# Attention with a modulated norm, followed by a GRU, on one core: the first part loads by halves of the features and projects q and k of batch 0 by contraction chunks

## The chip, the cores and the metric

The kernel runs on 1 core of a Trainium2 chip. The metric is the device time of one execution in microseconds (us); the number that counts is the median over several runs. Nothing else runs on the chip. All data are float32.

## The reference

There are 16 batches of 256 steps with 512 features, a condition vector of 512 features for each batch, and two layers one after the other.

```python
# layer 0: RMS norm, scaled and shifted by the condition, then attention with 16 heads of 32
scale, shift = split(cond @ W_emb + b_emb)           # W_emb: 512 x 1024
xn  = rms_norm(x, g_norm) * (1 + scale) + shift
q, k, v = split(xn @ W_qkv)                          # W_qkv: 512 x 1536
q, k = rms_norm_per_head(q, g_q), rms_norm_per_head(k, g_k)
o   = softmax(q @ k.T * 32**-0.5) @ v
x   = x + o + o @ W_out
# layer 1: GRU over the 256 steps, its first state is the condition
r = sigmoid(i_r + h_r); z = sigmoid(i_z + h_z); n = tanh(i_n + r * h_n)
h = (1 - z) * n + z * h                              # i = x_t @ W_ih + b_ih, h_* = h @ W_hh + b_hh
out = x + all h
```

## The kernel before

The program has three parts. The **first part** (lines 573 to 660) loads weights and x, makes scale and shift from the condition, and takes batch 0 as far as the start of its attention. The **attention part** loops over the batches 0 to 14 and, in each, over four groups of four heads; one group is one slot (`slot0` to `slot3`), and `last_batch` does batch 15. The **GRU part** runs over the 256 steps. Between the first two parts there is no barrier: the first logits of batch 0 (`logits`, line 285) are the border.

TensorE (PE), VectorE (DVE), ScalarE (ACT) and GpSimd (POOL) execute in the order in which the code is written (`manual_schedule`, line 571), each in its own queue. Each instruction waits for the semaphores of what it needs and holds up everything behind it on its engine. Loads are issued from the queues of SyncE (SP) and of ACT. The loads share eight semaphores in rotation, so that a load waits, before it is issued, until the load that last used its semaphore has landed; loads behind it on its queue wait with it.

What happens to one batch b, with the names that the change touches:

- `load_x(b)` loads x of the batch, 512 KB. The tile has two buffers.
- `norm_first(b)` takes squares and their sum on ACT, one instruction for each of the two halves of the steps (n = 0, 1). The squares themselves are a by-product, written into `xs`. `Rsqrt.first` and `Rsqrt.second` make 1/sqrt out of the sum: Ln and Exp on ACT, then a refinement of three small DVE instructions.
- `norm_apply(b)` writes the normed x into `xs` (DVE, two instructions); then `load_x(b + 2)` is issued.
- `turn_x(b)` transposes `xs` on PE into two PSUM banks, 16 instructions; `put_x` applies scale and shift (`ada_a`, `ada_s`) on the way to `xnT`, one bank by DVE and one by ACT or DVE.
- `project(b, n, s, ks)` multiplies `xnT` by `wq`: half n of the steps, s = 0, 1, 2 for q, k, v, over the contraction chunks ks of 128 features. One call over all four chunks appears in the profile as 32 matmuls (two for each instruction) at line 220. The result takes one PSUM bank.
- `Stats.square` and `Stats.add` square q or k (ACT) and sum by heads (DVE, line 235); `norm_qk` scales (DVE, line 246), `turn_qk` transposes on PE (line 194), `put_qk` writes qT and kT (lines 267 and 269), `put_v` keeps v.

There are eight PSUM banks, A, X, Y, Z and lg0 to lg3; `logits` needs lg0 to lg3. A bank that is given to a new tile waits until the last reader of the old one is done.

In the first part before, the queue of SP holds half of `we` (W_emb, 2 MB in all; ACT's queue holds the other half), x of batch 0, q's columns of `wq` (1 MB), four small rows, k's columns, x of batch 1, v's columns. PE's order is: turn the condition, all of `ps_emb` (the product of condition and `we`, line 587), turn x of batch 0, q and k of half 0, turn x of batch 1, q and k of half 1, with the turning of half 0's q and k and of x of batch 2 behind them, v of half 0, the turning of half 1's q and k, a quarter of v of half 1, the first logits.

Of the kernel before, what the change touches and what calls it, by code (L numbers as in the profile page):

```python
# [8 lines left out]
F32 = mybir.dt.float32  # L9
AF = mybir.ActivationFunctionType  # L10
# [9 lines left out]
def kernel(  # L20
# [52 lines left out]
    for k in range(KC):  # L73
        nc.scalar.dma_start(cond_sb[k * B : (k + 1) * B, :], cond[:, k * P : (k + 1) * P])
# [16 lines left out]
    we = wpool.tile([P, KC, 2 * D], F32, tag="w_a", name="we")  # L91
    for k in range(KC):
        (nc.sync, nc.scalar)[k % 2].dma_start(we[:, k, :], w_emb[k * P : (k + 1) * P, :])
# [3 lines left out]
    def load_x(b):  # L97
        xt = p2.tile([P, NT, D], F32, tag="x", name=f"x_{b}")
        nc.sync.dma_start(xt, x[b].rearrange("(n p) d -> p n d", p=P))
        x_tiles[b] = xt  # L100
# [3 lines left out]
    rows_b = p1.tile([26, P], F32, tag="qkn", name="rows_b", bufs=4)  # L104

    wq = wpool.tile([P, KC, 3 * D], F32, tag="w_b", name="wq")
    for i in range(3):
        for k in range(KC):
            nc.sync.dma_start(
                wq[:, k, i * D : (i + 1) * D], w_qkv[k * P : (k + 1) * P, i * D : (i + 1) * D]  # L110
            )
        if i == 0:
            for r, g in ((0, g_q), (1, g_k)):
                nc.sync.dma_start(
                    rows_b[r : r + 1, :].rearrange("o (i d) -> o i d", d=DH),
                    g.rearrange("(o i d) -> o i d", o=1, i=1).to_broadcast([1, HG, DH]),
                )
            nc.sync.dma_start(rows_b[2:14, :], b_ih.rearrange("(m c) -> m c", c=P))
            nc.sync.dma_start(rows_b[14:26, :], b_hh.rearrange("(m c) -> m c", c=P))
        if i == 1:  # L120
            load_x(1)
# [9 lines left out]
    def tile_ps(name, bank, shape=(P, D)):  # L131
        pool = ps if len(bank) == 1 else ps_lg
        return pool.tile(list(shape), F32, tag=bank, name=name)
# [31 lines left out]
    def norm_first(b, parts=range(NT)):  # L165
        if parts[0] == 0:
            batches[b].xs = p1.tile([P, NT, D], F32, tag="xs", name=f"xs_{b}")
            batches[b].ssx = small.tile([P, NT], F32, tag="ssx", name=f"ssx_{b}")
            batches[b].rs = Rsqrt(batches[b].ssx, D, NT, f"x{b}")
        for n in parts:  # L170
            nc.scalar.activation(
                batches[b].xs[:, n, :], x_tiles[b][:, n, :], AF.Square,
                accum_out=batches[b].ssx[:, n : n + 1],
            )

    def norm_apply(b, rstd):
        for n in range(NT):
            nc.vector.tensor_scalar(
                batches[b].xs[:, n, :], x_tiles[b][:, n, :], rstd[:, n : n + 1],
                None, ALU.mult,  # L180
            )
        batches[b].xnT = p1.tile([P, KC, T], F32, tag="xnT", name=f"xnT_{b}", bufs=2)
        if 0 < b and b + 2 < B:
            load_x(b + 2)
# [52 lines left out]
    def put_v(b, n, a):  # L237
        if n == 0:
            batches[b].v = p2.tile([P, NT, D], F32, tag="v", name=f"v_{b}")
        nc.scalar.copy(batches[b].v[:, n, :], a)  # L240
# [150 lines left out]
    def slot0(b, w, prev, st):  # L391
        m = b + 1
        if b == 0:

            project(b, 1, 2, range(1, KC), st.v1)
            maxima(w, range(HG))
            exps(w, range(HG))
            put_v(b, 1, st.v1)
            st.q = project(m, 0, 0, range(KC), "A")
            for r in range(R):  # L400
                put_x(2, r, st.tpx)
            st.s0 = Stats(m, 0)
            st.s0.add(0, st.s0.square(0, st.q))
            st.k = project(m, 0, 1, (0, 1), "X")
            normalize(w)
            return
# [164 lines left out]
    with tc.manual_schedule(engines=ORDERED):  # L571
# [6 lines left out]
        pe = tile_ps("ps_emb", "Z", (P, 8 * 32))  # L578
        nc.vector.memset(pe, 0.0)
        tp = tile_ps("tp_h0", "X", (P, KC, B))  # L580
# [4 lines left out]
        for k in range(KC):  # L585
            for j in range(4):
                nc.tensor.matmul(
                    pe[32 * j : 32 * j + B, :],
                    h0T[:, k, :],
                    we[:, k, :].rearrange("p (m j c) -> p j m c", j=4, c=32)[:, j],  # L590
                    start=(k == 0),
                    stop=(k == KC - 1),
                )
        tp = tile_ps("tp_rows", "Y")
        nc.tensor.transpose(tp[:, :12], rows, ident[:12, :12])
        norm_first(0)
        batches[0].rs.first()
        norm_apply(0, batches[0].rs.second())
        nc.vector.tensor_copy(cols[:, :12], tp[:, :12])
        emb = p1.tile([P, 8, 32], F32, tag="sq", name="emb")  # L600
        nc.vector.transpose(emb.rearrange("p m b -> p (m b)"), pe)
        nc.vector.tensor_tensor(
            emb[:, :, 0:B], emb[:, :, 0:B], cols[:, 0:8].unsqueeze(2).to_broadcast([P, 8, B]),
            ALU.add,
        )
        nc.vector.scalar_tensor_tensor(
            ada_a, emb[:, 0:KC, 0:B], 1.0, cols[:, 8:12].unsqueeze(2).to_broadcast([P, KC, B]),
            ALU.add, ALU.mult,
        )
        nc.vector.tensor_copy(ada_s, emb[:, KC:, 0:B])  # L610
# [6 lines left out]
        tpx = turn_x(0, "AX")  # L617
        for c in range(KC):
            put_x(0, 0, tpx, (c,))
            put_x(0, 1, tpx, (c,), nc.scalar)  # L620
        norm_first(1)
        batches[1].rs.first()
        norm_apply(1, batches[1].rs.second())
        q = project(0, 0, 0, range(KC), "Y")
        k = project(0, 0, 1, range(KC), "Z")
        tpx = turn_x(1, ("lg0", "lg1"))
        tp = tile_ps("tp_rows_b", "lg3")
        nc.tensor.transpose(tp[:, :26], rows_b, ident[:26, :26])
        nc.vector.tensor_copy(cols[:, 12:], tp[:, :26])
# [5 lines left out]
        s0 = Stats(0, 0)  # L635
        s0.add(0, s0.square(0, q))
        put_x(1, 1, tpx, engine=nc.scalar)
        s0.add(1, s0.square(1, k))
        s0.rs.first()
        put_x(1, 0, tpx)  # L640
        norm_first(2)
        qk = norm_qk(0, 0, (q, k), s0.rs.second())
        batches[2].rs.first()
        q = project(0, 1, 0, range(KC), "A")
        s1 = Stats(0, 1)
        s1.add(0, s1.square(0, q))
        norm_apply(2, batches[2].rs.second())
        k = project(0, 1, 1, range(KC), "X")
        tq = turn_qk(0, 0, qk, ("lg0", "lg1"))
        st.tpx = turn_x(2, "YZ")  # L650
        v = project(0, 0, 2, range(KC), "lg2")
        s1.add(1, s1.square(1, k))
        s1.rs.first()
        put_qk(0, 0, tq, nc.vector)
        put_qk(0, 1, tq, nc.scalar)
        put_v(0, 0, v)
        qk = norm_qk(0, 1, (q, k), s1.rs.second())
        tq = turn_qk(0, 1, qk, ("lg0", "lg1"))
        st.v1 = project(0, 1, 2, (0,), "X")
        put_qk(1, 0, tq, nc.vector)  # L660
        put_qk(1, 1, tq, nc.scalar)

# [293 lines left out]
```

## Time and profile before

| | us |
|---|---|
| median of 3 runs (1765.43 to 1771.71) | 1770.87 |
| the profiled execution | 1754.42 |
| its span, first to last instruction | 1752.6 |
| PE busy | 1729.9 (99%) |
| DVE busy | 1056.8 (60%) |
| ACT busy | 739.5 (42%) |
| start of the first product with `wq` | 16.55 |
| start of the first logits | 40.93 |

The span is one execution by the hardware profiler. "Busy" counts the time in which an engine has an instruction under way. PEld is the loading of weights into the array, which overlaps the matmuls. The chain of waits follows the work back from the last instruction to what released each step; an engine that this chain never leaves sets the time.

### The profile page before, as it was taken

What the parts mean: (1) busy time and instruction counts of PE and PEld (TensorE: products, weight loads), DVE (VectorE), ACT (ScalarE), POOL (GpSimd) and SP (SyncE); (2) the same over time, 40 slices, a digit from 0 to 9 for tenths busy, and PEclk for the clock granted to TensorE, in tenths of its full rate; (3) what the DMA queues carried; (4) which work ended last, traced back from release to release, by engine and by line L of the source; (5) the groups of instructions that cost most, each with busy time, mean ns of one, the idle gap of its engine ahead of it and who ended that gap; (6) DMA issues with size and microseconds to landing.
All of it is one profiled execution on the core that took longest, in us unless ns stands there. A gap on an engine that the chain in (4) does not pass through costs nothing.

```text
span 1752.6 us, 103775 instructions
## 1 busy us (share of the span) xinstructions
PE 1729.9 (99%) x46955; PEld 1355.0 (77%) x46955; DVE 1056.8 (60%) x3324; ACT 739.5 (42%) x2690; POOL 315.5 (18%) x773
## 2 busy tenths in 40 slices
PE   7999999999999999999999999999999999999998
PEld 2444444444444589999999999999999999999997
DVE  4777777777776745555555555555555555555554
ACT  3777777777777722222222222222222222222222
POOL 0344443444334410000000000000000000000000
PEclk9999999999999899999999999999999999999999
DMA  8100000000000111101110111011101100000000
GB/s 287 28 14 14 14 27 14 14 14 14 14 2 2 73 28 20 19 17 19 24 19 17 21 23 18 17 21 22 19 17 21 24 17 17 16 11 11 11 16 16
DMA packets 146266, 44.48 MB, mean 25 GB/s; under 512 B 137899, under 2 KB 138031, under 8 KB 145823
## 3 DMA queue, kind: packets, MB, share of 16 engines
q1 hardware_dynamic: 145351, 36.73, 9.2%
q8 instruction: 368, 6.03, 1.4%
q10 hardware_dynamic: 472, 1.10, 0.2%
q14 instruction: 75, 0.61, 0.1%
HBM read 29.41 MB, written 8.39 MB: 22 GB/s over the span
## 4 chain that ended last, share of the span: by engine, by line
PE 96%; DVE 2%; ACT 1%; DMA 1%; issue 0%; DVEq 0%; ACTq 0%
PE qkv L220 19%; PE gn L775 19%; PE gr L775 19%; PE gz L775 19%; PE o L719 6%; PE lg L285 4%; PE tpa L194 4%; PE o L364 4%; PE tpqk L194 1%; ACT attn L307 1%; PE tpx L194 1%; PE first L520 0%; DMA x<-in_x_dram 0%; DMA we<-in_L_cond_W_emb_dram 0%; DVE trh L799 0%
## 5 line engine op out<-in xcount | busy, mean ns | idle before, releaser
L220 PE MATMUL qkv<-wq,xnT 128*32 128x512 f32 x3072 | 357.6, 600 | 0.6 <-DVE xnT L212 0.6
L318 POOL TENSOR_SCALAR attn<-attn,rden 128x256 f32<-128x256 f32 x510 | 232.8, 478 | 383.1 <-DVE rden L315 262.9
L873 ACT ACTIVATE r<-trr 128x64 f32<-128x64 f32 x256 | 65.4, 256 | 515.6 <-DVE trr L799 515.6
L307 ACT ACTIVATE attn<-lg,neg 128x256 f32<-128x256 f32 x512 | 234.4, 483 | 67.8 <-DVE neg L301 45.1
L799 DVE STREAM_TRANSPOSE trr<-gr 128x128 f32<-128x128 f32 x256 | 81.1, 317 | 247.5 <-PE gr L775 247.4
L220 PEld LDWEIGHTS qkv<-wq,xnT 128*32 128x32 f32 x3072 | 87.6, 110 | 183.4 <-issue 158.9
L877 ACT ACTIVATE n<-n 128x64 f32<-128x64 f32 x256 | 65.7, 257 | 309.8 <-DVE n L876 306.8
L301 DVE TENSOR_REDUCE neg<-lg 128x2 f32<-128x512 f32 x256 | 159.2, 684 | 50.4 <-PE lg L285 50.4
L799 DVE STREAM_TRANSPOSE trh<-gn 128x128 f32<-128x128 f32 x256 | 81.1, 317 | 142.2 <-PE gn L775 142.2
L775 PE MATMUL gn<-wih,xT 128*32 128x128 f32 x4096 | 159.7, 273 | 0.0
L719 PE MATMUL o<-oT,wo 128*32 128x256 f32 x1920 | 148.0, 379 | 0.0
L775 PE MATMUL gr<-whh,padded 128*32 128x128 f32 x4096 | 135.9, 273 | 2.3 <-DVE padded L906 1.4
L908 POOL TENSOR_TENSOR y<-xT,padded 128x64 f32<-128x64 f32 x128 | 41.0, 321 | 533.5 <-DVE padded L906 533.5
L775 PE MATMUL gr<-wih,xT 128*32 128x128 f32 x4096 | 136.1, 273 | 0.0
L775 PEld LDWEIGHTS gn<-wih,xT 128*32 128x32 f32 x4096 | 120.4, 110 | 20.3
L775 PE MATMUL gz<-wih,xT 128*32 128x128 f32 x4096 | 136.0, 273 | 0.0
L775 PE MATMUL gz<-whh,padded 128*32 128x128 f32 x4096 | 135.8, 273 | 0.0
L775 PE MATMUL gn<-whh,padded 128*32 128x128 f32 x4096 | 135.7, 273 | 0.0
L775 PE MATMUL gr<-whh,h 128*16 128x128 f32 x4064 | 134.6, 273 | 0.3
L775 PE MATMUL gz<-whh,h 128*16 128x128 f32 x4064 | 134.2, 273 | 0.2
L775 PE MATMUL gn<-whh,h 128*16 128x128 f32 x4064 | 134.2, 273 | 0.0
L775 PEld LDWEIGHTS gr<-wih,xT 128*32 128x32 f32 x4096 | 117.4, 110 | 20.5
(122 smaller groups left out, 2731.4 us busy)
## 6 DMA issues: line engine op xcount, KB each, us to landing
x<-in_x_dram SPq DMA_DIRECT2D x16, 512.0 KB, 4.0
xin<-in_x_dram SPq DMA_DIRECT2D x256, 32.0 KB, 2.5
out_dram<-osb SPq DMA_DIRECT2D x248, 32.0 KB, 1.9
wq<-in_L_cond_W_qkv_dram SPq DMA_DIRECT2D x12, 256.0 KB, 4.8
wih<-in_L_cond_W_ih_dram SPq DMA_DIRECT2D x4, 768.0 KB
whh<-in_L_cond_W_hh_dram SPq DMA_DIRECT2D x4, 768.0 KB
we<-in_L_cond_W_emb_dram SPq DMA_DIRECT2D x2, 512.0 KB, 4.8
we<-in_L_cond_W_emb_dram ACTq DMA_DIRECT2D x2, 512.0 KB
```

The costliest lines, as they stand in the source:

```text
L194: nc.tensor.transpose(dst[r], src[q], ident[q, q])
L220: nc.tensor.matmul(a[32 * j : 32 * j + 32, :], batches[b].xnT[:, k, n * P + 32 * j : n * P + 32 * j + 32], wq[:, k, s * D : (s + 1) * D], ...
L285: nc.tensor.matmul(w.lg[i][:, n, :], qT[r, g, n * P : (n + 1) * P], kT[r, g, :], start=True, stop=True,)
L301: nc.vector.tensor_reduce(w.neg[:, i, :], w.lg[i], AX.X, ALU.max, negate=True)
L307: nc.scalar.activation(a[:, n, :], w.lg[i][:, n, :], AF.Exp, bias=w.neg[:, i, n : n + 1], accum_out=w.den[:, i, n : n + 1],)
L318: engine.tensor_scalar(w.attn[i][:, n, :], w.attn[i][:, n, :], w.rden[:, i, n : n + 1], 1.0, ALU.mult, ALU.mult,)
L364: nc.tensor.matmul(w.o[i * DH : (i + 1) * DH, :], v[:, k, h * DH : (h + 1) * DH], w.attnT[:, i, k, :], start=(k == 0), stop=(k == NT - 1),)
L719: nc.tensor.matmul(acc[32 * j : 32 * j + 32, :], w[:, k, m * P + 32 * j : m * P + 32 * j + 32], rhs, start=(k == 0), stop=(k == KC - 1),)
L775: nc.tensor.matmul(dst[32 * j : 32 * j + rows, :], stationary, w[:, k, g * D : (g + 1) * D].rearrange("p (q j c) -> p j q c", q=KC, c=32)[ ...
L799: nc.vector.transpose(tr.rearrange("p q s b -> p (q s b)"), gate)
L873: nc.scalar.activation(r, turned("r", t, gr[:, 0, :])[:, :, s, :], AF.Sigmoid)
L877: nc.scalar.activation(n, n, AF.Tanh)
```

## The change

The loads of the first part are reordered. The condition comes by both queues, x of batch 0 is the first large load of SP, and the four small rows go to ACT's queue. `we` is loaded in two halves of its columns (features 0 to 255 of scale and of shift, then 256 to 511), each in four loads of 256 KB. Behind each half come two of the four contraction chunks of `wq` for q and k together (512 KB each); then x of batch 1, then v's columns.

Scale and shift are made in two halves too (`embed(0)`, `embed(1)`), and after each the two chunks of x that it serves are put into `xnT`. x of batch 0 is turned ahead of `embed(0)`. q and k of both halves of the steps are kept in four banks at once and projected chunk by chunk (`q_and_k`). v of half 0 follows, and then the statistics, norms and turns of all four, batch 1's norm among them. x of batch 1 is turned last, into lg0 and lg1, right ahead of the first logits, and put into `xnT` by DVE and ACT. The norm of x of batch 2 is applied, and x turned and put, in `slot0` of batch 0; its squares go to two borrowed buffers. Without its blank lines:

```diff
--- before.py
+++ after.py
@@ -71,7 +71,9 @@
     cond_sb = const.tile([KC * B, P], F32, name="cond_sb")
     for k in range(KC):
-        nc.scalar.dma_start(cond_sb[k * B : (k + 1) * B, :], cond[:, k * P : (k + 1) * P])
+        (nc.scalar, nc.sync)[k % 2].dma_start(
+            cond_sb[k * B : (k + 1) * B, :], cond[:, k * P : (k + 1) * P]
+        )
     h0T = const.tile([P, KC, B], F32, name="h0T")
     cols = const.tile([P, 38], F32, name="cols")
@@ -88,9 +90,14 @@
     rows = p1.tile([12, P], F32, tag="qkn", name="rows", bufs=4)
     nc.scalar.dma_start(rows[0:8, :], b_emb.rearrange("(m c) -> m c", c=P))
     nc.scalar.dma_start(rows[8:12, :], g_norm.rearrange("(m c) -> m c", c=P))
-    we = wpool.tile([P, KC, 2 * D], F32, tag="w_a", name="we")
-    for k in range(KC):
-        (nc.sync, nc.scalar)[k % 2].dma_start(we[:, k, :], w_emb[k * P : (k + 1) * P, :])
+    rows_b = p1.tile([26, P], F32, tag="qkn", name="rows_b", bufs=4)
+    for r, g in ((0, g_q), (1, g_k)):
+        nc.scalar.dma_start(
+            rows_b[r : r + 1, :].rearrange("o (i d) -> o i d", d=DH),
+            g.rearrange("(o i d) -> o i d", o=1, i=1).to_broadcast([1, HG, DH]),
+        )
+    nc.scalar.dma_start(rows_b[2:14, :], b_ih.rearrange("(m c) -> m c", c=P))
+    nc.scalar.dma_start(rows_b[14:26, :], b_hh.rearrange("(m c) -> m c", c=P))
     x_tiles = {}
@@ -101,24 +108,21 @@
     load_x(0)
-    rows_b = p1.tile([26, P], F32, tag="qkn", name="rows_b", bufs=4)
+    we = wpool.tile([P, KC, 2 * D], F32, tag="w_a", name="we")
     wq = wpool.tile([P, KC, 3 * D], F32, tag="w_b", name="wq")
-    for i in range(3):
+    for i in range(2):
         for k in range(KC):
+            c = slice(i * (D // 2), (i + 1) * (D // 2))
             nc.sync.dma_start(
-                wq[:, k, i * D : (i + 1) * D], w_qkv[k * P : (k + 1) * P, i * D : (i + 1) * D]
+                we[:, k, :].rearrange("p (h c) -> p h c", h=2)[:, :, c],
+                w_emb[k * P : (k + 1) * P, :].rearrange("p (h c) -> p h c", h=2)[:, :, c],
             )
-        if i == 0:
-            for r, g in ((0, g_q), (1, g_k)):
-                nc.sync.dma_start(
-                    rows_b[r : r + 1, :].rearrange("o (i d) -> o i d", d=DH),
-                    g.rearrange("(o i d) -> o i d", o=1, i=1).to_broadcast([1, HG, DH]),
-                )
-            nc.sync.dma_start(rows_b[2:14, :], b_ih.rearrange("(m c) -> m c", c=P))
-            nc.sync.dma_start(rows_b[14:26, :], b_hh.rearrange("(m c) -> m c", c=P))
-        if i == 1:
-            load_x(1)
+        for k in range(2 * i, 2 * i + 2):
+            nc.sync.dma_start(wq[:, k, 0 : 2 * D], w_qkv[k * P : (k + 1) * P, 0 : 2 * D])
+    load_x(1)
+    for k in range(KC):
+        nc.sync.dma_start(wq[:, k, 2 * D :], w_qkv[k * P : (k + 1) * P, 2 * D :])
@@ -162,18 +166,23 @@
     batches = [Batch() for _ in range(B)]
-    def norm_first(b, parts=range(NT)):
+    def norm_first(b, parts=range(NT), squares=None):
         if parts[0] == 0:
-            batches[b].xs = p1.tile([P, NT, D], F32, tag="xs", name=f"xs_{b}")
             batches[b].ssx = small.tile([P, NT], F32, tag="ssx", name=f"ssx_{b}")
             batches[b].rs = Rsqrt(batches[b].ssx, D, NT, f"x{b}")
+            if squares is None:
+                batches[b].xs = squares = p1.tile([P, NT, D], F32, tag="xs", name=f"xs_{b}")
+        elif squares is None:
+            squares = batches[b].xs
         for n in parts:
             nc.scalar.activation(
-                batches[b].xs[:, n, :], x_tiles[b][:, n, :], AF.Square,
+                squares[:, n % squares.shape[1], :], x_tiles[b][:, n, :], AF.Square,
                 accum_out=batches[b].ssx[:, n : n + 1],
             )
     def norm_apply(b, rstd):
+        if b == 2:
+            batches[b].xs = p1.tile([P, NT, D], F32, tag="xs", name=f"xs_{b}")
         for n in range(NT):
             nc.vector.tensor_scalar(
                 batches[b].xs[:, n, :], x_tiles[b][:, n, :], rstd[:, n : n + 1],
@@ -395,10 +404,12 @@
             project(b, 1, 2, range(1, KC), st.v1)
             maxima(w, range(HG))
             exps(w, range(HG))
+            norm_apply(2, batches[2].rs.second())
             put_v(b, 1, st.v1)
             st.q = project(m, 0, 0, range(KC), "A")
+            tpx = turn_x(2, "YZ")
             for r in range(R):
-                put_x(2, r, st.tpx)
+                put_x(2, r, tpx)
             st.s0 = Stats(m, 0)
             st.s0.add(0, st.s0.square(0, st.q))
             st.k = project(m, 0, 1, (0, 1), "X")
@@ -575,90 +586,117 @@
-        pe = tile_ps("ps_emb", "Z", (P, 8 * 32))
+        pe = tile_ps("ps_emb", "Z", (P, 2, P))
         nc.vector.memset(pe, 0.0)
-        tp = tile_ps("tp_h0", "X", (P, KC, B))
+        tp = tile_ps("tp_h0", "lg2", (P, KC, B))
         nc.tensor.transpose(
             tp.rearrange("p k b -> p (k b)"), cond_sb, ident[: KC * B, : KC * B]
         )
         nc.vector.tensor_copy(h0T, tp)
-        for k in range(KC):
-            for j in range(4):
-                nc.tensor.matmul(
-                    pe[32 * j : 32 * j + B, :],
-                    h0T[:, k, :],
-                    we[:, k, :].rearrange("p (m j c) -> p j m c", j=4, c=32)[:, j],
-                    start=(k == 0),
-                    stop=(k == KC - 1),
-                )
-        tp = tile_ps("tp_rows", "Y")
+        tp = tile_ps("tp_rows", "lg3")
         nc.tensor.transpose(tp[:, :12], rows, ident[:12, :12])
+        nc.vector.tensor_copy(cols[:, :12], tp[:, :12])
+        b_cols = cols[:, 0:8].rearrange("p (h m) -> p h m", h=2)
         norm_first(0)
         batches[0].rs.first()
         norm_apply(0, batches[0].rs.second())
-        nc.vector.tensor_copy(cols[:, :12], tp[:, :12])
-        emb = p1.tile([P, 8, 32], F32, tag="sq", name="emb")
-        nc.vector.transpose(emb.rearrange("p m b -> p (m b)"), pe)
-        nc.vector.tensor_tensor(
-            emb[:, :, 0:B], emb[:, :, 0:B], cols[:, 0:8].unsqueeze(2).to_broadcast([P, 8, B]),
-            ALU.add,
-        )
-        nc.vector.scalar_tensor_tensor(
-            ada_a, emb[:, 0:KC, 0:B], 1.0, cols[:, 8:12].unsqueeze(2).to_broadcast([P, KC, B]),
-            ALU.add, ALU.mult,
-        )
-        nc.vector.tensor_copy(ada_s, emb[:, KC:, 0:B])
+        def embed(i):
+            for k in range(KC):
+                for j in range(4):
+                    nc.tensor.matmul(
+                        pe[32 * j : 32 * j + B, i, :],
+                        h0T[:, k, :],
+                        we[:, k, :].rearrange("p (h m j c) -> p j h m c", h=2, j=4, c=32)[
+                            :, j, :, 2 * i : 2 * i + 2
+                        ],
+                        start=(k == 0),
+                        stop=(k == KC - 1),
+                    )
+            emb = small.tile([P, 2, 2, 32], F32, tag="emb", name=f"emb_{i}", bufs=1)
+            m = slice(2 * i, 2 * i + 2)
+            nc.vector.transpose(emb.rearrange("p h m b -> p (h m b)"), pe[:, i, :])
+            bias = [b_cols[:, h, m].unsqueeze(2).to_broadcast([P, 2, B]) for h in range(2)]
+            nc.vector.tensor_tensor(emb[:, 0, :, 0:B], emb[:, 0, :, 0:B], bias[0], ALU.add)
+            nc.vector.scalar_tensor_tensor(
+                ada_a[:, m], emb[:, 0, :, 0:B], 1.0,
+                cols[:, 8 + 2 * i : 10 + 2 * i].unsqueeze(2).to_broadcast([P, 2, B]),
+                ALU.add, ALU.mult,
+            )
+            nc.vector.tensor_tensor(ada_s[:, m], emb[:, 1, :, 0:B], bias[1], ALU.add)
+        def put_x0(c):
+            put_x(0, 0, tpx, (c,))
+            put_x(0, 1, tpx, (c,), nc.scalar)
+        def q_and_k(k, halves=range(NT)):
+            for n in halves:
+                for i in range(2):
+                    accs[n][i] = project(0, n, i, (k,), accs[n][i])
+        tpx = turn_x(0, ("lg0", "lg1"))
+        embed(0)
+        put_x0(0)
+        put_x0(1)
+        accs = [["A", "X"], ["lg2", "lg3"]]
+        q_and_k(0)
+        q_and_k(1, (0,))
+        embed(1)
+        q_and_k(1, (1,))
+        put_x0(2)
+        put_x0(3)
+        q_and_k(2)
+        q_and_k(3)
         load_x(2)
         nc.sync.dma_start(wo, w_out.rearrange("(k p) n -> p k n", p=P))
         wih = wpool.tile([P, KC, 3 * D], F32, tag="w_a", name="wih")
         for k in range(KC):
             nc.sync.dma_start(wih[:, k, :], w_ih[k * P : (k + 1) * P, :])
-        tpx = turn_x(0, "AX")
-        for c in range(KC):
-            put_x(0, 0, tpx, (c,))
-            put_x(0, 1, tpx, (c,), nc.scalar)
-        norm_first(1)
+        v = project(0, 0, 2, range(KC), "Y")
+        s0, s1 = Stats(0, 0), Stats(0, 1)
+        s0.add(0, s0.square(0, accs[0][0]))
+        s0.add(1, s0.square(1, accs[0][1]))
+        norm_first(1, (0,))
+        s0.rs.first()
+        s1.add(0, s1.square(0, accs[1][0]))
+        rstd = s0.rs.second()
+        s1.add(1, s1.square(1, accs[1][1]))
+        norm_first(1, (1,))
+        s1.rs.first()
         batches[1].rs.first()
-        norm_apply(1, batches[1].rs.second())
-        q = project(0, 0, 0, range(KC), "Y")
-        k = project(0, 0, 1, range(KC), "Z")
-        tpx = turn_x(1, ("lg0", "lg1"))
-        tp = tile_ps("tp_rows_b", "lg3")
+        qk = norm_qk(0, 0, accs[0], rstd)
+        rstd = s1.rs.second()
+        squares = [
+            p1.tile([P, 1, D], F32, tag="attn", name=f"squares_{n}", bufs=8) for n in range(NT)
+        ]
+        norm_first(2, (0,), squares[0])
+        tp = tile_ps("tp_rows_b", "lg0")
         nc.tensor.transpose(tp[:, :26], rows_b, ident[:26, :26])
+        tq = turn_qk(0, 0, qk, "AX")
+        st.v1 = project(0, 1, 2, (0,), "Z")
+        qk = norm_qk(0, 1, accs[1], rstd)
         nc.vector.tensor_copy(cols[:, 12:], tp[:, :26])
         bcols = cols[:, 14:38]
         nc.vector.tensor_tensor(bcols[:, 0:8], bcols[:, 0:8], bcols[:, 12:20], ALU.add)
         nc.vector.tensor_scalar(gq_col, cols[:, 12:13], DH ** -0.5, None, ALU.mult)
         nc.vector.tensor_copy(gk_col, cols[:, 13:14])
-        s0 = Stats(0, 0)
-        s0.add(0, s0.square(0, q))
-        put_x(1, 1, tpx, engine=nc.scalar)
-        s0.add(1, s0.square(1, k))
-        s0.rs.first()
-        put_x(1, 0, tpx)
-        norm_first(2)
-        qk = norm_qk(0, 0, (q, k), s0.rs.second())
-        batches[2].rs.first()
-        q = project(0, 1, 0, range(KC), "A")
-        s1 = Stats(0, 1)
-        s1.add(0, s1.square(0, q))
-        norm_apply(2, batches[2].rs.second())
-        k = project(0, 1, 1, range(KC), "X")
-        tq = turn_qk(0, 0, qk, ("lg0", "lg1"))
-        st.tpx = turn_x(2, "YZ")
-        v = project(0, 0, 2, range(KC), "lg2")
-        s1.add(1, s1.square(1, k))
-        s1.rs.first()
         put_qk(0, 0, tq, nc.vector)
         put_qk(0, 1, tq, nc.scalar)
-        put_v(0, 0, v)
-        qk = norm_qk(0, 1, (q, k), s1.rs.second())
-        tq = turn_qk(0, 1, qk, ("lg0", "lg1"))
-        st.v1 = project(0, 1, 2, (0,), "X")
+        norm_first(2, (1,), squares[1])
+        batches[2].rs.first()
+        norm_apply(1, batches[1].rs.second())
+        tq = turn_qk(0, 1, qk, ("lg2", "lg3"))
+        tpx = turn_x(1, ("lg0", "lg1"))
         put_qk(1, 0, tq, nc.vector)
         put_qk(1, 1, tq, nc.scalar)
+        put_x(1, 0, tpx)
+        put_x(1, 1, tpx, engine=nc.scalar)
+        put_v(0, 0, v)
         prev = None
         for b in range(B - 1):
```

## The prediction

> **What bounds the kernel now.** I read the page's engine shares first, then the chain of waits of the first 45 us, then the timeline of weight loads in the same stretch, and last the table of windows for a later place where PE (TensorE) has little to do.
>
> The engine shares, and from the chain of waits (start, length, what):
>
> ```profile
> PE 1729.9 (99%) x46955; PEld 1355.0 (77%) x46955; DVE 1056.8 (60%) x3324; ACT 739.5 (42%) x2690; POOL 315.5 (18%) x773
> ```
>
> ```profile
> 0.74 3.87 DMA we<-in_L_cond_W_emb_dram
> 4.62 6.81 DMA x<-in_x_dram
> ...
> 16.55 9.57 PE qkv L220 x64
> 26.12 0.69 PE tpx L194 x16
> ...
> 35.65 3.57 PE qkv L220 x32
> 39.22 0.65 PE tpqk L194 x16
> 39.87 1.00 PE qkv L220 x8
> 40.87 0.06 issue
> 40.93 1.15 PE lg L285 x16
> ```
>
> The chain enters through two loads; from 16.55 us PE is busy without a real break, and later waits are small. So the time is PE's work behind the first logits, plus when they start: whatever moves 40.93 us moves the end by the same amount. The chain goes through DVE (VectorE) and ACT (ScalarE) at 26 to 34 us without PE stopping: q and k of half 1 cover the norms of half 0, and v covers those of half 1.
>
> The timeline of weight loads shows PE's pace (start, duration of one; four loads belong to four matmuls of 512 columns):
>
> ```profile
> 19.97 0.21 PEld L220 LDWEIGHTS qkv<-wq,xnT 128*32 128x32 f32 x4 [0.64 <-issue]
> 20.82 0.21 PEld L220 LDWEIGHTS qkv<-wq,xnT 128*32 128x32 f32 x4 [0.64 <-issue]
> 21.65 0.13 PEld L220 LDWEIGHTS qkv<-wq,xnT 128*32 128x32 f32 x4 [0.61 <-issue]
> 22.08 0.13 PEld L220 LDWEIGHTS qkv<-wq,xnT 128*32 128x32 f32 x4 [0.30 <-issue]
> ```
>
> Four take 0.85 us up to 21.6 and 0.43 us after. PE starts at half pace, though the clock column of these windows says 1.00, and needs 5.05 us of unbroken products to get out of it. The windows before the last batch show how it falls back (window, its length, PE busy; the third number from the end is the granted clock):
>
> ```profile
> 591.60:595.00 3.40, 2.57 (x28) 1.52 (x25) 3.22 (x7) 3.14 (x14) 1.21 (x4) 1.00 1.00 412
> 595.00:598.40 3.40, 3.40 (x20) 1.62 (x23) 1.47 (x3) 2.25 (x9) 2.98 (x7) 0.51 1.01 420
> 598.40:601.90 3.50, 3.50 (x46) 2.45 (x40) 2.23 (x5) 2.25 (x11) 0.00 (x0) 0.50 0.01 2
> ```
>
> A window with PE busy for 2.57 of 3.40 us is followed by 6.8 us at half clock.
>
> **The change, step by step.** All times are us in the profiled execution.
>
> *A. To the first product.* x of batch 0 is now SP's third load. SP issues one in 0.45, so at 1.65; the first large load of before took 3.87, so it lands near 5.5 (before: 11.4). The small rows moved to ACT's queue come ahead of its table load there (5.36 before, 1.28 long), and three wait for an earlier landing; I put the table's end at 6.5 and the squares there. From the squares (11.45) to the first turn (14.52) the row is 3.07: 9.6; the turns took 1.41 at half pace: 11.0. `embed(0)` now stands behind them. The whole product was 3.8 busy with 256 columns; half the columns cost between 1.9 and 3.8, I take 2.7: 13.7. From the transpose of `ps_emb` (14.85) to the first product (16.55) it is 1.70: start at 15.4 instead of 16.55. The four loads of the first half of `we` are needed by 11.0. I estimate the last at 10.5, since the third waits for x's landing and x and this half are 1.5 MB at 345 GB/s (window 5 to 10). That cover is thin; without it each us late costs one.
>
> *B. q and k of batch 0, both halves.* 64 matmuls took 7.07 at full pace (26.86), a chunk of 8 thus 0.88; 16 chunks are 14.1. `embed(1)` stands among them, half of 2.7 at full pace: 1.35. It removes nothing, since before it had run ahead of 16.55. The 5.05 at half pace come again: +2.5. End: 15.4 + 14.1 + 1.35 + 2.5 = 33.3. The remaining loads are hidden: before, x of batch 1, behind 4.5 MB of weights, was squared at 20.56, and PE wants the second half of `we` only near 23.
>
> *C. The norms, now with little above them.* q of half 0 is complete at 30.7, because the chunk order finishes all four only in the last round. `sq` has one buffer, so squares (ACT, 0.60) and sums (DVE, 0.68) alternate: four pairs are 5.3, and half 0's Ln, Exp and refinement among them 0.7: 36.7. Then DVE has in its queue: two small means 0.33; scalings of half 0 1.29; refinement 0.6; scalings of half 1 1.29; five small copies 0.65; put_qk 0.88; a wait of 0.5 for ACT, whose second square for batch 2 stands behind its own put_qk; mean and refinement for batch 1 0.75; `norm_apply(1)` 0.88; put_qk 0.88; `put_x` of batch 1 1.4. Sum 9.4: 46.1. The logits can't start earlier, because lg0 and lg1 hold the turned x of batch 1 until `put_x` has read them. The same addition over the old order ends 0.3 too late, which I take off: 45.8 against 40.93, **+4.8**. PE has below this v 3.57, three turns 2.1 and a quarter of v 1.0, ends its v at 36.9 and waits some 6 of the 9 us left.
>
> *D. Slot 0.* The turn of x of batch 2 (0.69) leaves the part ahead of the logits, which C has counted, and stands in slot 0 on PE: **+0.7**. DVE gets 1.5 more there (refinement 0.6, `norm_apply(2)` 0.88), and `put_x` now follows the turn, so the reciprocal for POOL comes about 2 us into slot 1. PE turns there 5.5 behind the logits (49.87 to 55.37); POOL's 3.65 fits, hence nothing; were it late, under 1.
>
> *E. The clock.* From 36.9 to 45.8 PE works a third of the time, far below the 2.57 of 3.40 that cost the clock above. At half pace the first products of slot 0 lose half of 3.4 to 6.8 us; with 5.05 as at the start, **+2.5**. [...] The window at 591.6 was three quarters busy and lost the clock, so the trace decides for E.
>
> *F. Moved loads.* x of batch 3 is issued at its `norm_apply(1)`, near 44 instead of 24, x of batch 4 near 51 instead of 35, each between `xin` loads on SP; first need is the squares in slot 1 (57.15 before), and x lands in 4.0 by the page's row. Hidden by 9 us; the `xin` loads behind them belong to the GRU part. `wih` waits for `embed(1)`: also GRU. Nothing.
>
> Sum: 4.8 + 0.7 + 2.5 = 8.0. The profiled execution has 1754.4, so 1762.4; the median of the runs shown is 16.5 above it, and I add the same 8.0: 1778.9, or +0.45%.
>
> **Rivals.**
> 1. *The clock is kept through the gap.* Against it: the windows above. 1770.9 + 5.5 = 1776.4.
> 2. *The tail hides, not slower.* If DVE and ACT did the norms while PE still projects, PE alone would count: 15.4 + 24.4 (16.55 to 40.93) - 0.7 + 1.35 = 40.4, with D +0.2: 1771.1; with the clock raised already by turns and `embed(0)` 2.5 less, 1768.6. It decides if the tail behind the last product is under PE's 6.7; by the rows it is 12.5. For it: loads do come earlier.
> 3. *The front loads come late.* Before, x took 6.81 to land. Landing at 8.5, it would delay the squares by 2.0 and the rest of the first half of `we` behind it on SP. It decides from a landing near 7.5; price up to 2.0, plus up to 0.9 where the clock rises late: 1781.8.
>
> **How the numbers follow.** Half a per cent (8.9 us) is about what a measurement of this kernel can tell from no change, and the forecast ends just within it. Its sizes vary: the half pace at the start and in E by 0.9 each, A by 1, C by 1, the run median by 2. Chances: the forecast 0.78, of which 0.36 beyond 8.9 and 0.42 within; rival 1 0.11, within; rival 3 0.07, beyond; rival 2 0.04, half of it given to faster (it would need PE's own work to shrink). Faster 0.02, same 0.55, slower 0.43. Range: rival 1 less 0.9, 1 and 1 gives 1773.5; rival 3 with 3 of the sizes above gives 1785.
>
> **What would show it.** Right: first product near 15.4; q and k done near 33; PE idle for about 6 us between 37 and 46, released by DVE's `qkn`, `xs` and `xnT`; logits near 46; weight loads of slot 0 at 0.85 per four for some us. Wrong: logits before 43, or full pace right behind them; or a gap on `we` or `wq` among the products.

## The result, and the profile after

| | before | after |
|---|---|---|
| median, 5 runs each on one chip | 1770.18 (1765.43 to 1771.71) | 1779.29 (1776.85 to 1779.92) |
| profiled execution (its span) | 1754.42 (1752.6) | 1779.29 (1777.5) |
| first product with `wq` | 16.55 | 14.01 |
| first logits, second logits | 40.93, 49.87 | 43.15, 55.24 |
| first to last sigmoid of r in the GRU part | 1111.7 | 1132.9 |

The medians lie 9.1 us apart. The ratio of after to before on record is 1.0044 with an interval of 1.0024 to 1.0064, which is 7.8 us. By either number after is slower by about half a per cent. The profiled executions lie 24.9 apart, but 21.2 of that is the GRU part, which the change doesn't touch; the experiments show it to be scatter. In the shares PE still has almost the whole span:

```profile
PE 1744.0 (98%) x46987; PEld 1368.8 (77%) x46987; DVE 1057.2 (59%) x3328; ACT 739.6 (42%) x2690; POOL 315.5 (18%) x773
```

The chain of waits of after (start, length, what) enters by ACT's queue instead of by a load of weights, and between 28 and 43 us it now belongs to ACT and DVE, but for the turn of x of batch 1 on PE (0.83):

```profile
4.97 1.28 ACT L584
6.29 0.51 issue
6.80 0.81 ACT xs L178 x3
...
9.32 0.37 PE tpx L203
...
10.73 1.88 PE ps_emb L608 x32
...
12.63 0.33 DVE emb L619
...
14.01 6.99 PE qkv L229 x48
20.99 0.87 PE ps_emb L608 x32
21.87 6.04 PE qkv L229 x56
27.93 0.61 ACT sq L240
...
39.87 0.89 DVE xs L187 x2
40.81 0.83 PE tpx L203 x14
41.64 1.37 DVE xnT L221 x4
43.15 2.21 PE lg L294 x16
45.35 7.45 PE qkv L229 x56
52.81 0.65 PE tpx L203 x16
```

No load stands in it behind the first product. In before, this stretch was PE from 35.0 to the logits. What PE waits for between 33 and 44 us (us in total, times, longest):

```profile
PE tpx L203 <- DVE xs L187: 2.3, 1, 2.3
PE lg L294 <- DVE xnT L221: 1.5, 1, 1.5
PE tpqk L203 <- DVE qkn L255: 0.9, 1, 0.9
PE tpqk L203 <- DVE u_qk L157: 0.4, 1, 0.4
```

That is 5.1 us, of which 4.7 by the three releasers that the prediction named (`xs`, `xnT`, `qkn`) and 0.4 by `u_qk`, a step of the norm of half 1. Then the clock. Windows laid along its changes, the outer ones half as long as the 6.83 at half clock between them (window, length, PE busy; third number from the end the granted clock):

```profile
37.73:41.14 3.41, 0.99 (x25) 0.71 (x22) 2.69 (x10) 2.67 (x8) 0.00 (x0) 1.00 0.02 5
41.14:47.97 6.83, 5.28 (x44) 2.51 (x42) 4.47 (x12) 4.00 (x14) 0.00 (x0) 0.50 0.46 103
47.97:51.38 3.41, 3.41 (x40) 0.94 (x36) 1.04 (x3) 2.21 (x9) 0.00 (x0) 1.00 0.25 53
```

PE has 0.99 us of work in the 3.41 ahead of the fall, and the logits and the first of slot 0 run at half pace. The first logits take 2.21 instead of 1.15, and the weight loads behind them are 0.85 apart until 47.85 and 0.43 after, as predicted:

```profile
46.99 0.20 PEld L229 LDWEIGHTS qkv<-wq,xnT 128*32 128x32 f32 x4 [0.66 <-issue]
47.85 0.18 PEld L229 LDWEIGHTS qkv<-wq,xnT 128*32 128x32 f32 x4 [0.66 <-issue]
48.34 0.12 PEld L229 LDWEIGHTS qkv<-wq,xnT 128*32 128x32 f32 x4 [0.31 <-issue]
48.77 0.12 PEld L229 LDWEIGHTS qkv<-wq,xnT 128*32 128x32 f32 x4 [0.31 <-issue]
```

### The profile page after: what moved, and what is told of

It is laid out like the page before. It is cut to its first block, busy times and chain, and to the rows that moved or that the text cites. A ratio compares the mean times of both kernels' runs of the same rounds, so it can differ in the third digit from the quotient of the medians.

```text
span 1777.5 us, 103845 instructions
## 1 busy us (share of the span) xinstructions
PE 1744.0 (98%) x46987; PEld 1368.8 (77%) x46987; DVE 1057.2 (59%) x3328; ACT 739.6 (42%) x2690; POOL 315.5 (18%) x773
## 4 chain that ended last, share of the span: by engine, by line
PE 96%; DVE 2%; ACT 1%; issue 1%; ACTq 0%; DVEq 0%
PE qkv L229 19%; PE gr L813 19%; PE gn L813 19%; PE gz L813 19%; PE o L757 6%; PE lg L294 4%; PE tpa L203 4%; PE o L373 4%; PE tpqk L203 1%; PE tpx L203 1%; ACT attn L316 1%; PE first L531 0%; DVE trh L837 0%; DVE ssqk L244 0%; PE ps_emb L608 0%
## 5 line engine op out<-in xcount | busy, mean ns | idle before, releaser
L813 PE MATMUL gn<-wih,xT 128*32 128x128 f32 x4096 | 165.1, 273 | 0.3
L757 PE MATMUL o<-oT,wo 128*32 128x256 f32 x1920 | 152.9, 380 | 1.4 <-issue 1.2
L813 PEld LDWEIGHTS gn<-wih,xT 128*32 128x32 f32 x4096 | 128.1, 110 | 16.4 <-issue 1.4
L813 PE MATMUL gz<-whh,padded 128*32 128x128 f32 x4096 | 139.9, 273 | 0.7 <-issue 0.3
L813 PE MATMUL gr<-wih,xT 128*32 128x128 f32 x4096 | 139.8, 273 | 0.6
L813 PE MATMUL gn<-whh,padded 128*32 128x128 f32 x4096 | 139.6, 273 | 0.6
L813 PE MATMUL gz<-wih,xT 128*32 128x128 f32 x4096 | 139.6, 273 | 0.4
L813 PE MATMUL gz<-whh,h 128*16 128x128 f32 x4064 | 137.8, 273 | 1.0 <-issue 0.9
L813 PEld LDWEIGHTS gr<-wih,xT 128*32 128x32 f32 x4096 | 122.1, 110 | 17.8 <-issue 1.6
```

Source lines behind the costliest of these rows:

```text
L757: nc.tensor.matmul(acc[32 * j : 32 * j + 32, :], w[:, k, m * P + 32 * j : m * P + 32 * j + 32], rhs, start=(k == 0), stop=(k == KC - 1),)
L813: nc.tensor.matmul(dst[32 * j : 32 * j + rows, :], stationary, w[:, k, g * D : (g + 1) * D].rearrange("p (q j c) -> p j q c", q=KC, c=32)[ ...
```

## The experiments

The theory: the front is earlier, but the norms of batch 0 no longer lie below PE's products; the uncovered tail (C) and the clock lost in its gap (E) outweigh the earlier start. Rivals: the loss lies in the GRU part or in moved loads; the clock costs nothing. The kernels ran in three groups, each on another chip together with before (before_again, after_again, filler and oldloads; v1gap, halves, x1early and best; the rest). The milestones of all profiles, in us ("half clock" is the start and length of a stretch, without those in the last batch and in the last 6 us of the program; the GRU column as above):

| kernel | first product | logits 1 | logits 2 | half clock | GRU part |
|---|---|---|---|---|---|
| before / after (first pair) | 16.55 / 14.01 | 40.93 / 43.15 | 49.87 / 55.24 | none / 41.1, 6.8 long | 1111.7 / 1132.9 |
| before_again | 15.66 | 39.80 | 48.73 | none | 1117.8 |
| after_again | 13.88 | 41.41 | 53.58 | 39.6, 6.8 | 1116.1 |
| filler | 13.89 | 42.69 | 52.52 | none | 1116.4 |
| oldloads | 20.00 | 47.47 | 59.90 | 46.1, 6.8 | 1115.1 |
| v1gap | 13.98 | 43.71 | 52.35 | none | 1120.3 |
| halves | 13.90 | 39.47 | 51.13 | 36.6, 6.8 | 1127.4 |
| x1early | 13.89 | 45.00 | 54.72 | 26.1, 3.4 | 1127.1 |
| best | 13.89 | 47.57 | 56.23 | 24.6, 6.8 | 1128.9 |
| x1late | 13.90 | 40.81 | 51.99 | 40.5, 3.4 | 1129.0 |
| halves_v1 | 13.90 | 41.53 | 50.17 | none | 1135.3 |
| best2 | 13.89 | 40.59 | 49.26 | none | 1137.6 |
| after_third | 13.89 | 43.16 | 55.46 | 41.6, 6.8 | 1139.4 |

### The same kernels again: before_again, after_again, after_third

No edit.

> The kernel before, unchanged. Theory 1 (the change costs 5.4 us, all of it ahead of the second logits of batch 0, and the rest of the 9.1 us between the medians is scatter of the GRU part): this kernel's own GRU part, from the first to the last sigmoid of r, takes other values than the 1111.7 us of its first profile, somewhere up to 1132.9 as in the profile of the changed kernel, while the first logits stay at 40.9 +- 1 and the second at 49.9 +- 1. Theory 2 (the change slows the GRU part too): the GRU part stays near 1112 here and is near 1133 in each profile of the changed kernel.

> The changed kernel, unchanged. Theory 1: first product near 14, first logits near 43.2, second near 55.2 within 2 us (the clock's free moment), GRU part anywhere between 1112 and 1133 us; the median of many rounds 4 to 8 us above the kernel before. Theory 2: GRU part again 1133 +- 3 us.

> The changed kernel once more, for the scatter of its parts: first logits 41.4 to 43.2, half clock for 6.8 us from 39 to 41, second logits 53.5 to 55.3; the GRU part anywhere between 1112 and 1133 us if its length is scatter of the run, near 1133 if the 21 us of the first profile belong to the change.

before_again: 1754.53 over 12 runs, ratio to before 1.0003 (0.9993 to 1.0012). Its first and second logits, 39.80 and 48.73, lie just below the ranges given. after_again: 1764.06 over 5 runs, 9.3 above before's median on this chip where 4 to 8 was expected; the ratio is 1.0057 (1.0044 to 1.0070), which is 10.0. The GRU part of after took 1132.9, 1116.1 and 1139.4 in three profiles, and on the chip of the second one that of before took 1117.8, longer than after's. On the chip of the third, before's median was 1780.1 (1754.8 and 1765.3 on the others), and two kernels with other first parts had 1135.3 and 1137.6 there: the 21 us of the first pair belong to the chip and the run. The median step of the GRU part is 4.36 us in every profile; what differs is how many of the 255 steps take over 4.42, from 9 (before) to 93 (after_third), with 31 in before_again and 25 in after_again. after_third missed the range that was given for the GRU part, upwards, and by 0.2 the one for logits 2. The three profiles of after agree from logits 1 to logits 2, 12.1 to 12.3.

Their logits 1 lie between 41.4 and 43.2, and that spread comes from the clock. Its first recorded rise is at 17.25, 12.28 and 17.68, and q of half 0 is complete at 27.93, 26.26 and 28.08. Products that run ahead of the rise run at half pace (in the first profile the weight loads are 0.85 apart up to 17.25 and 0.43 behind it), so half of the time from the first product to the rise is lost: 1.6, nothing and 1.9. In the two profiles of before the rise is at 21.60 and 19.34, and the logits are 1.1 apart, half of that difference.

The granted clock is on record for every run, and splits the timed difference in two. I multiply its shortfall from 1 by the run's time and take the mean on the chip of after_again. The 17 runs of before have a clock of 0.9962 on average and lose 6.7 of their 1755.0 us; the 5 of after_again have 0.9934 and lose 11.6 of 1763.9. So of the difference of the means, 9.0, some 4.9 (standard error 0.8) is clock and 4.0 (1.0) is not. This counts half clock also where PE was idle, and the record has three decimals, 1.8 us for one run.

### The load order alone: oldloads

After's compute with the loads as before had them (order, sizes and queues).

```diff
+    for k in range(KC):
+        (nc.sync, nc.scalar)[k % 2].dma_start(we[:, k, :], w_emb[k * P : (k + 1) * P, :])
     load_x(0)
-    for i in range(2):
+    for i in range(3):
         for k in range(KC):
-            ... # half i of we[:, k, :], then two chunks of wq for q and k
+            nc.sync.dma_start(
+                wq[:, k, i * D : (i + 1) * D], w_qkv[k * P : (k + 1) * P, i * D : (i + 1) * D]
+            )
+        if i == 0: ... # small rows
+        if i == 1: load_x(1)
```

> The order of the loads of the kernel before (W_emb first on both queues, x behind it, q's, k's, v's columns) under the new order of the computation. If the loads are what brings the first product forward: squares of x at 11.4, first product near 19 instead of 14.0, first logits near 47 instead of 43.2. Rival (the new order of PE alone brings it forward, the loads are hidden anyway): first product at 14 to 15.

The first product came at 20.00 instead of 13.88, the logits at 47.47 instead of 41.41. The new order brings the front 6.1 us forward within this compute order. Without it the change would cost some 6 us more.

### The clock in the gap: filler, v1gap

filler puts four products of one chunk each, whose result is not used, into the gap (`fill`) and the quarter of v behind the turn of x:

```diff
+        fill()
         tq = turn_qk(0, 0, qk, "AX")
-        st.v1 = project(0, 1, 2, (0,), "Z")
+        fill()
...
         tq = turn_qk(0, 1, qk, ("lg2", "lg3"))
+        fill()
+        fill()
         tpx = turn_x(1, ("lg0", "lg1"))
+        st.v1 = project(0, 1, 2, (0,), "Z")
```

> Four needless products of one chunk (0.88 us each, result never read) stand in the gap of PE ahead of the first logits, the real quarter of v follows them. Theory of the clock: the granted clock stays at 1.00 after 40 us, the first logits start at 43.2 +- 0.7 as before and take 1.1 instead of 2.2 us, and the second logits come near 53 instead of 55.2. Rival (slot 0 is longer because of the norm and turn of batch 2 that the change put there, not because of the clock): the second logits stay near 55.2, 12 us behind the first.

PE in filler's timeline (start, length):

```profile
37.72 1.92 PE L683 MATMUL junk<-wq,xnT 128*32 128x512 f32 x16
40.10 1.04 PE L203 MATMUL tpx<-ident,xs 64*128 64x64 f32 x16 [0.46 <-DVE xs L187]
...
42.69 1.26 PE L294 MATMUL lg<-kT,qT 32*128 32x256 f32 x16 [0.56 <-DVE xnT L221]
```

With 3.5 us more of PE's work ahead of them the logits come 15.1 behind q of half 0, as in after (15.1 to 15.2), so PE's own work isn't what they wait for. The clock stays at 1.00, and from logits 1 to logits 2 it is 9.83 instead of 12.09 to 12.30: E is worth 2.3 to 2.5 us.

v1gap fills the gap with useful work: the other three quarters of v of half 1, which slot 0 then lacks.

```diff
-        st.v1 = project(0, 1, 2, (0,), "Z")
+        st.v1 = project(0, 1, 2, (0, 1), "Z")
...
         tq = turn_qk(0, 1, qk, ("lg2", "lg3"))
+        project(0, 1, 2, (2, 3), st.v1)
# slot0
-            project(b, 1, 2, range(1, KC), st.v1)
```

> The last three quarters of v of half 1 move from slot 0 into PE's gap ahead of the first logits (2.65 us of products). If PE's gap is true idle time, the first logits stay at 43.2 +- 0.7 and the second come 2.7 us earlier, at 52.6, or near 50.5 if the fuller gap also keeps the clock. Rival (PE is not what slot 0 waits for): second logits at 55 as before.

The clock is kept, and logits 2 come at 52.35, 2.9 earlier than in the first profile of after (1.2 than in after_again); logits 1 at 43.71. The three chunks are 2.6 of PE's work, but slot 0 got only 1.2 shorter than filler's (8.64 against 9.83): PE now waits 1.1 there for ACT's copy of v, ahead of the turn of x of batch 2. So the 50.5 that was expected with the clock kept did not come.

```profile
49.86 0.71 PE L203 MATMUL tpx<-ident,xs 64*128 64x64 f32 x15 [1.08 <-ACT v L249]
```

### What stands above the tail: halves, x1early, x1late

halves finishes q and k of half 0 before those of half 1, and scales half 0 before half 1's sums:

```diff
-        q_and_k(0)
+        q_and_k(0, (0,))
         q_and_k(1, (0,))
         embed(1)
-        q_and_k(1, (1,))
+        q_and_k(0, (1,))
         put_x0(2)
         put_x0(3)
-        q_and_k(2)
-        q_and_k(3)
+        q_and_k(2, (0,))
+        q_and_k(3, (0,))
+        for k in range(1, KC):
+            q_and_k(k, (1,))
...
         rstd = s0.rs.second()
+        qk = norm_qk(0, 0, accs[0], rstd)   # was behind s1.rs.first()
```

> q and k of half 0 are finished over all four chunks before half 1 goes on, and half 0 is normed ahead of half 1's sums. If finishing all four in the last round is what leaves the norms uncovered, half 0's norms now run under half 1's products and the first logits come 2 to 3.5 us earlier, 40 to 41. Rival (the end of the tail is set by batch 1's norm, turn and put, whatever is ahead of it): first logits within 1 us of 43.2.

PE in halves (start, length, idle before):

```profile
36.52 1.41 PE L203 MATMUL tpx<-ident,xs 64*128 64x64 f32 x16 [1.82 <-DVE xs L187]
39.47 2.21 PE L294 MATMUL lg<-kT,qT 32*128 32x256 f32 x16 [1.55 <-DVE xnT L221]
```

Logits 1 came at 39.47, 1.9 earlier than in after_again, whose clock rose as early as here (12.3 and 12.7 us); 2 to 3.5 was expected. So part of C is the chunk order, which holds back half 0 until the last round. The gap before the turn of x of batch 1 remains, the clock fell at 36.6, and logits 2 were late all the same (51.13).

x1early takes the norm, turn and put of x of batch 1 out of the tail: norm ahead of `q_and_k(0)`, turn and put within `q_and_k(2)`.

```diff
         accs = [["A", "X"], ["lg2", "lg3"]]
+        load_x(2)
+        norm_first(1)
+        batches[1].rs.first()
+        norm_apply(1, batches[1].rs.second())
         q_and_k(0)
...
-        norm_apply(1, batches[1].rs.second())
-        tpx = turn_x(1, ("lg0", "lg1"))
```

> Norm, turn and put of batch 1 move ahead, under the products of batch 0, so lg0 and lg1 are free early and DVE has 2.9 us less behind the last product. If this part of DVE's queue is on the path, the first logits come 2.5 to 3.5 us earlier, 39.7 to 40.7. Rival (the alternation of squares and sums and half 1's norm set the end): within 1 us of 43.2.

The tail got shorter as expected: from q of half 0 (32.47) to the logits 12.5 instead of 15.2. The logits were late, at 45.00, by my placement. x of batch 1 lands at 20.8, and its norm held up DVE ahead of `embed(1)`'s chain:

```profile
23.35 0.88 DVE L187 TENSOR_SCALAR xs<-x,y_x 128x512 f32<-128x512 f32 x2
24.14 0.31 DVE L619 STREAM_TRANSPOSE emb<-ps_emb 128x128 f32<-128x128 f32 x1
...
25.51 3.15 PE L229 MATMUL qkv<-wq,xnT 128*32 128x512 f32 x16 [3.58 <-DVE xnT L221]
```

PE waited 3.58 for `xnT` and lost the clock there (26.1). x1late mends this: the norm goes behind `put_x0(3)`, the turn ahead of the last chunk of half 1, and one chunk of `put_x` behind each of the four sums.

```diff
         put_x0(3)
-        q_and_k(2)
-        q_and_k(3)
         load_x(2)
+        norm_first(1)
+        batches[1].rs.first()
+        norm_apply(1, batches[1].rs.second())
+        q_and_k(2)
+        q_and_k(3, (0,))
+        tpx = turn_x(1, ("lg0", "lg1"))
+        q_and_k(3, (1,))
...
         s0.add(0, s0.square(0, accs[0][0]))
+        put_x(1, 0, tpx, (0,))
+        put_x(1, 1, tpx, (0,), nc.scalar)
```

> After with one move only: x of batch 1 squared and normed behind embed(1)'s DVE chain (about 24 us, x of batch 1 landed at 20.8), turned on PE ahead of the last chunk of half 1, put in chunks between the sums. Theory: the tail is the sum of DVE's and ACT's work, so norm, turn and put of batch 1 (0.75 + 0.88 + 1.4, of which about 2.7 seen in the first try) leave it: from q of half 0 complete to the first logits 12.5 instead of 15.25, q of half 0 complete at 28 to 28.5, first logits 41 +/- 0.7. Rival: the tail is one chain of waits through half 1's q and k that x of batch 1 only fills: still 15, first logits 43.

Logits 1 at 40.81, against 43.15 in the first profile of after, whose clock rose about as early (17.3 and 16.6 us); from the first square of q (27.56) it is 13.2. That lies between 12.5 and 15, nearer the first: work moved out of the tail shortens it, by 2.0 of the 2.7 expected. The logits now wait for half 1's k (`kT`, ACT) and no longer for `xnT`. The clock still fell, for 3.4 us.

```profile
40.81 2.09 PE L294 MATMUL lg<-kT,qT 32*128 32x256 f32 x16 [2.42 <-ACT kT L276]
```

### Put together: best, halves_v1, best2

best is halves, x1early and v1gap with x1early's flaw; halves_v1 is halves and v1gap; best2 adds to halves_v1 the norm of batch 1 where x1late has it, with its turn between the chunks of half 1 and its put among half 1's sums (not shown here):

```diff
         put_x0(3)
         load_x(2)
+        norm_first(1)
+        batches[1].rs.first()
+        norm_apply(1, batches[1].rs.second())
         q_and_k(2, (0,))
         q_and_k(3, (0,))
         q_and_k(1, (1,))
+        tpx = turn_x(1, ("lg0", "lg1"))
         q_and_k(2, (1,))
         q_and_k(3, (1,))
```

> All three together: halves one after the other, batch 1 put under the products, all of v of half 1 in the gap. If the uncovered tail and the lost clock are the whole cost of the change: first logits 39 to 40.5 with v done, clock kept, second logits 46.5 to 48.5 against 49.9 in the kernel before, start of the GRU part 1 to 4 us earlier than before, median of runs 0 to 4 us below the kernel before. Rival (something else in the change costs time): second logits after 50.

> As best2, but x of batch 1 stays where the change has it (norm and turn at the end of the tail). By halves and v1gap measured one by one: first logits 40.1 (39.47 + 0.56 for v), second logits 48.2 to 49, no half clock between 30 and 47 because the gap is filled; time within 2 us of before, 6 to 9 below after. Rival, that the halves alone open a gap in which the clock falls whatever stands in it: half clock for 6.8 us near 36, second logits near 51, time 3 us above before.

> q and k by halves of the steps, half 0 normed first, all of v of half 1 ahead of the first logits (slot 0 loses it), and x of batch 1 squared and normed behind the DVE chain of embed(1), turned among the products of half 1 and put in chunks between the sums of half 1. If the length of the uncovered tail behind the last product is what the change costs (C) and the gap the clock (E): first logits 39 +/- 1 with v of half 1 complete, no stretch at half clock between 30 and 47, second logits near 47.5 (before: 48.7 to 49.9; after: 53.6 to 55.2); time 6 to 9 us below after and 0 to 3 us below before (ratio to before 0.998 to 1.000). Rival, that the timed difference of 9 us lies behind the first part (the moved loads, the attention or GRU part): second logits near 47.5 all the same, but the time stays 3 us or more above before (ratio 1.002 to 1.004).

best: 1772.07 over 12 runs, ratio 1.0035 (1.0018 to 1.0052), logits 1 at 47.57: the flaw again, so the expectation failed. halves_v1: no half clock, logits at 41.53 and 50.17, each over a microsecond later than I said; ratio 0.9994 (0.9970 to 1.0018). best2: PE runs without a break from the first product to behind the first logits:

```profile
28.48 7.00 PE qkv L229 x64
35.66 0.65 PE tpqk L203 x16
36.30 1.85 PE qkv L229 x16
38.16 0.65 PE tpqk L203 x14
38.80 1.85 PE qkv L229 x16
40.66 1.11 PE lg L294 x16
```

Its logits come at 40.59 (39 ± 1 expected) and 49.26 (47.5 expected). From one to the other it is 8.67, near the 8.5 expected, although slot 0 waits 1.2 for ACT's copy of v as in v1gap. Most of the lateness, in halves_v1 too, is the start: the clock rose at 19.02 and 17.93 there, but at 12.72 in halves. The ratio is 0.9983 (0.9958 to 1.0008), 1776.67 against 1780.06. So neither is shown to beat before, but neither shows a loss: with the tail covered and the gap filled, the new load order costs nothing that can be measured, and gains nothing either. Their GRU parts (1135.3 and 1137.6) are as long as after_third's on the same chip; what they lack is the gap and its clock.

## Why the prediction was right, and where its sizes were off

The range and the likeliest case held: 1778.9 forecast, 1779.29 measured. The mechanism held too: a tail of norms on ACT and DVE that PE waits for, and the clock lost in its gap. The sum behind the number held less well.

**A** was too late by 1.4: first product at 14.01, not 15.4. `embed(0)` took 1.9, half of the whole product's 3.8 (2.7 assumed), the turn began 0.3 earlier, and from the transpose of `ps_emb` to the first product it was 1.4 instead of 1.70. PE didn't wait for `we`: `embed(0)` followed the turn without a gap. So rival 3 is out.

**B**: half pace lasted 3.2 us behind the first product, not 5.05, and cost 1.6 instead of 2.5; in after_again, where the clock rose ahead of the first product, it cost nothing. What sets the moment of the rise no run here tests. `embed(1)` took 0.87 instead of 1.35. With A this puts v's end at 33.81 instead of 36.9.

**C** has the right length and place: from q of half 0 to the logits 15.2, predicted 15.1, with PE waiting 5.1 (some 6 predicted), nearly all for the releasers named. So rival 2, the tail hidden under PE's work, is out. But it starts 2.8 earlier, so the logits moved by +2.2 (+1.6 between before_again and after_again), not +4.8 (45.8 less 40.93 is 4.87; the prediction rounded it down). The mis-sized terms are A's and B's, not the tail. The prediction called logits before 43 a sign that it was wrong; after_again's 41.41 is one, and means this miss.

**D** is nearly right (0.7): the turn in slot 0 took 0.65; with the clock kept, slot 0 is 0.9 longer (filler's 9.83 against 8.9 in both profiles of before).

**E** is right: 2.3 to 2.5, and rival 1 is out: the clock fell at 41.14, behind 3.41 us with PE busy for 0.99, and stayed at half for 6.83. The 3.4 at the lower end of E's stretch was my estimate, since the two stretches ahead of the last 6 us of before last 6.83 each (from 595.04 and 608.70); one of 3.41 came in after, from 614.58.

**F** and the rest: logits of batch 1 are 5.36 later than in before, as logits 2 were (5.37), and those of batch 15 are 5.31 later; in the second pair it is 4.85 at logits 2 and 4.80 at batch 15. So neither the moved loads of x nor anything else in the attention part up to there adds to the loss.

So the profiles give 5.4 (first pair) and 4.9 (second pair) up to logits 2, where the sum said 8.0, and the medians of the runs give 9.1 and 9.3 (the ratios 7.8 and 10.0). The total was met partly by luck: A to C were 2.6 too dear, and something that the sum lacks made up for it. For the second chip's 9.0 (difference of the means, standard error 1.0) the parts are: logits 1 later by 2.2 (mean of three profiles of after less that of two of before), D 0.9, E 2.4. By the granted clock another 1.5 is half clock outside the gap, since of the 4.9 the stretch in the gap makes half of 6.83. That is not settled: in the last batches after has 10.2 us at half clock and before_again 6.8, but before's first profile 13.7. About 2.0 stay without a place. The two shares that they come from have standard errors of 0.8 and 1.0, and the 2.2 rests on five profiles whose logits 1 differ by up to 1.8 within one kernel, so the 2.0 is not clear of nothing. Whatever of it is real lies behind the first logits of batch 15, or the profiles' first parts aren't typical of the timed runs; no run here decides.

## What to carry to other kernels

Splitting a contraction by chunks across several accumulators starts the products earlier but finishes all results together, and then little is left to cover the work behind the first of them; finish one half first (in halves the logits came 1.9 us earlier). Before moving a load or product forward, write down what the engine will run while the next stage's norms are made, since in after PE waited 5.1 us in the gap and the half clock behind it cost another 2.3 to 2.5 (E, against filler). Where a gap can't be avoided, work that is due soon anyway, moved into it, kept the clock here as well (v1gap, halves_v1, best2); and a norm moved forward must not stand ahead of a chain that PE waits for on the same queue (in x1early PE waited 3.58 us for it).

## What the runs showed of the hardware that was not expected

- The GRU part, the same instructions in every kernel here, took 1111.7 to 1139.4 us by chip and run. So a single profile can't resolve 5 us in 1770 at the end of the program; milestones in the first 60 us could.
- Share of busy time alone didn't decide the clock here. A window of 3.40 us with PE busy for 2.29 kept it in v1gap (from 42.60), and so did one with 1.85 (from 41.60); one of 3.41 with 2.90 lost it in after (from 611.17). Step E argued from such a share (2.57) and was right for a gap with 0.99; as a threshold it doesn't hold. What decides is not known.
- The clock's first recorded rise came at 12.3, 17.3 and 17.7 us in three profiles of the same kernel, and the stretches at half clock last 3.4 or 6.8 us (in after 6.83 from 41.14 and 3.41 from 614.58), once 17.1 (v1gap, last batch), where the end of the program doesn't cut them off.
